# Scores of eight heads at a time, and the attention products of the batch before in front

## The chip, the cores and the metric

The kernel runs on one core of a Trainium2 chip. A core has a matmul engine (TensorE, PE in the profile, with weight loads as PEld), a vector engine (VectorE, DVE), a scalar engine (ScalarE, ACT), a general one (GpSimd, POOL) and a queue that only issues transfers (SyncE, SP). Each engine takes its own instructions in order and waits on semaphores for what others produce. The metric is the time of one execution in microseconds (us), as the median of several runs. Instruction durations come from one profiled execution of the same program.

## The reference

There are 32 batches. Each has 100 rows of x with 256 features, and a context of 361 rows with 256 features. One layer is computed, in fp32 where not said otherwise.

```
xn  = layernorm(x)
Qh, Kh, Vh = xn WQ, ctx WK, ctx WV          # 16 heads of 64
attn = softmax(Qh Kh^T / 8 + mask * -1e9)   # mask 100 x 361, one for all batches
x   = x + concat_heads(attn Vh) WO
x   = x + qlinear(gelu(qlinear(layernorm(x), W1, b1)), W2, b2)
```

`qlinear` rounds its input to 8 bits with one scale and zero point taken over the whole tensor, and its weight to 8 bits with one scale. Hence the second part of the kernel can't begin before all 32 batches have left attention. F, the hidden width, is 1024.

## The kernel before

The program has two parts: attention over 32 batches one after the other, and then the FFN over all rows. The change is in attention alone.

**Tiling.** A "pair" is two heads: 128 rows of queries or keys. A batch has 8 pairs. Eight batch groups (g) of four batches (j = 0 to 3, b = 4g + j) share what is done once a group: the normalized rows (`ln1`, `ln1_T`), the queries (`q_part`, 32 matmuls at the end of j=3), the output projection of the group before (`project_T`, 32 matmuls at the end of j=0), and its transposing back (`project_back`, at the end of j=1 and j=2, followed on VectorE by the residual, statistics and extremes, and on GpSimd by a power and a store). `normalize` of these rows comes one batch later. In the last group each batch but the first is projected on its own (`project`).

**One batch's path.** `products` (L435) multiplies queries and keys of a head into a PSUM bank; two heads of a pair use two halves of the array's rows. `minima` (L449, VectorE) adds the mask, writes the scores to `pb` and finds each row's minimum (queries carry a minus sign). `exponentials` (L463, ScalarE) exponentiates in place and sums. `divide` (L471, L478, VectorE) multiplies by the reciprocal sums, four heads a call. `send` (L503, L512) has GpSimd copy a pair into one of two `apart` buffers with the 16-bit halves of each number taken apart, and SP issue a transposing DMA from there to one of three xT buffers. `join` (L519, ScalarE) puts the halves together again as pT. `attend` (L540) multiplies pT and the values, 96 small matmuls a batch, pair after pair, and ScalarE copies out its two banks (L547). `k_part` (L280, copied by ScalarE at L287) makes the next batch's keys of a pair, `v_part` (L311, copied by VectorE at L318) a third of half of this batch's values.

**Buffers.** PSUM is a ring of eight banks: each score product, key pair, value third and half of `attend` takes the next one, and waits until the one eight places earlier has been read. `pb` holds eight heads. pT, the keys and the values have one buffer each a batch.

**Order.** `whole_batch` is called for batches 1 to 30, and lists by hand the order for TensorE, VectorE, ScalarE and GpSimd; SP's order is found by the framework's planner. The first and the last batch go in parts (`part_of_batch`), transposing on TensorE (`weights_T`). Before the change a whole batch is four quarters (q) of two pairs: scores, minima, exponentials and the keys of two pairs of the next batch. The last join of the batch before stands in quarter 0, its `attend` behind quarter 1, and the values in quarters 2 and 3; the joins of a batch come two quarters behind its sends, the third one after `rest`, which holds the group's work named above. Pieces of the FFN's weight quantization (`todo`) are added in batches 1 to 10: two loads by DMA issued from GpSimd, maxima, rounding.

**Start.** GpSimd clears the last rows of the two `apart` buffers (L205) before it issues two small loads and computes the inverse deviations (L334, L335) that `ln1(0)` needs. VectorE scales two copies of the mask by 1e9 (L675, L676): one for batches in parts, `maskh`, and one for whole batches, `maskt`.

Of the kernel before, what the change touches and what calls it, by code (L numbers as in the profile page):

```python
# [12 lines left out]
ALU = mybir.AluOpType  # L13
# [14 lines left out]
def kernel(  # L28
# [133 lines left out]
    with ExitStack() as att:  # L162
# [38 lines left out]
            wpool.tile([TR, 2 * NSC * 2 * SC], I16, tag=f"apart{k}", name=f"apart{k}")  # L201
            for k in range(2)
        ]
        for t in apart:
            nc.gpsimd.memset(t[T // 32 * 32 :], 0.0)  # L205

        def bank(name):
            return psum.tile([P, 512], F32, tag="ps", name=name)
# [55 lines left out]
        def whole(i):  # L264
            return steps[i][2] == NHP
# [99 lines left out]
        def q_part(g, q):  # L365

            if g >= NG:
                return
            for pair in range(PAIRS):
                pq = bank(f"pq{g}_{q}_{pair}")  # L370
                for dc in range(NDC):
                    nc.tensor.matmul(  # L372
                        pq[:, :GT],
                        wqt[q][:, dc, pair * P : (pair + 1) * P],
                        xnTs[g][:, dc, :],
                        start=(dc == 0),
                        stop=(dc == NDC - 1),
                    )
                j0, j1 = 0, G
                if pair == 0 and g == NG - 1:  # L380
                    clear(q, G - 1)
                for j in range(G):
                    if halved(g * G + j):
                        j0, j1 = (1, G) if j == 0 else (0, j)
                        for k in range(2):
                            nc.vector.tensor_scalar(
                                qbuf[q][:, pair, j, k * RH : k * RH + TH],
                                pq[:, j * T + k * TH : j * T + (k + 1) * TH],
                                -1.0 / DK**0.5, None, ALU.mult,
                            )  # L390
                nc.vector.tensor_scalar(
                    qbuf[q][:, pair, j0:j1, :T],
                    pq[:, j0 * T : j1 * T].rearrange("p (j t) -> p j t", t=T),
                    -1.0 / DK**0.5, None, ALU.mult,
                )
# [30 lines left out]
        def products(i, pairs):  # L426


            b = steps[i][0]
            n = TP if halved(b) else T  # L430
            pss = {}
            for h in range(2 * pairs[0], 2 * pairs[-1] + 2):
                pair, k = divmod(h, 2)
                pss[h] = bank(f"sc{i}_{h}")[:n, :S]
                nc.tensor.matmul(  # L435
                    pss[h],
                    qbuf[pair // PAIRS][k * DK : (k + 1) * DK, pair % PAIRS, b % G, :n],
                    kT[k * DK : (k + 1) * DK, pair, :],
                    start=True,
                    stop=True,  # L440
                )
            return pss

        def minima(i, pss):

            for h, ps in pss.items():
                n = ps.shape[0]
                ms[h] = small.tile([TP, 1], F32, tag=f"m{h}", name=f"m{i}_{h}", bufs=1)
                done = nc.vector.tensor_tensor_reduce(  # L449
                    pb[:n, h % NB, :S], ps, maskh if halved(steps[i][0]) else maskt, 1.0, BIG,  # L450
                    ALU.add, ALU.min, ms[h][:n],
                )
            return done
# [13 lines left out]
        def divide(i, heads, at_once=4, after=None):  # L467
            rsum, r = sums[i]
            n = TP if halved(steps[i][0]) else T
            for h0 in heads[::at_once]:  # L470
                last = nc.vector.reciprocal(  # L471
                    r[:n, h0 : h0 + at_once], rsum[:n, h0 : h0 + at_once]
                )
                if after is not None:
                    follow(last, after)
                for h in range(h0, h0 + at_once):
                    s = pb[:n, h % NB, :S]
                    nc.vector.tensor_scalar(s, s, r[:n, h : h + 1], None, ALU.mult)  # L478
            return last
# [34 lines left out]
        def join(i, q):  # L514
            for pair in range(q * PAIRS, (q + 1) * PAIRS):
                pT = pTs[i, pair] = p1.tile(
                    [SC, 2 * NSC, T], F32, tag=f"pT{pair}", name=f"pT{i}_{pair}"
                )
                nc.scalar.copy(  # L519
                    pT.bitcast(I16).rearrange("s c (t l) -> s c t l", l=2),  # L520
                    xTs[i, pair][:, :, :T].rearrange("s (c l) t -> s c t l", l=2),
                )
# [150 lines left out]
        for b in range(G):  # L673
            stats1(b)
        nc.vector.tensor_scalar(maskh, maskh, 1e9, None, ALU.mult)  # L675
        nc.vector.tensor_scalar(maskt, maskt, 1e9, None, ALU.mult)  # L676
        warm(bank("warm0"), 7)
        k_start()
        for h in range(2):
# [2 lines left out]
        ln1(0)  # L682
        ln1_T(0)
        q_part(0, 0)

# [27 lines left out]
        def part_of_batch(i):  # L715


            b, first, n = steps[i]
            g, j = b // G, b % G
            begun = [h for h in range(2) if first <= h * HP < first + n]  # L720
            ended = [h for h in range(2) if first < (h + 1) * HP <= first + n]
            first_copied = None
            last = scores(i)
            if i >= 1:
                if whole(i - 1):
                    join(i - 1, NQ - 1)
                attend(i - 1)
            if b >= 1:
                for h in begun:
                    for c in range(NSC):  # L730
                        done = v_part(b, h, c)
                        if h == begun[0] and c == 0:
                            first_copied = done
                        if c != 2:
                            copied = done
            while later and i < len(steps) - 1:
                normalize(later.pop(), copied)
            if b == 0 and first < HP:
                for q in range(1, 2) if first == 0 else range(2, NQ):
                    q_part(0, q)  # L740
            rest(i, ended, last, first_copied)
            if g == NG - 1 and j >= 1 and 1 in begun:
                project(b - 1, range(NHP))
            if i + 1 < len(steps):
                for pair in range(steps[i + 1][2]):
                    k_part(i + 1, pair)

        def whole_batch(i):

            b = steps[i][0]
            g, j = b // G, b % G
            late = []
            if not whole(i - 1):
                for pair in range(steps[i - 1][1], steps[i - 1][1] + steps[i - 1][2]):
                    weights_T(i - 1, pair, True)
            for q in range(NQ):
                heads = range(2 * PAIRS * q, 2 * PAIRS * (q + 1))
                minima(i, products(i, range(q * PAIRS, (q + 1) * PAIRS)))  # L760
                if q == 1:
                    divide(i, range(2 * PAIRS))
                    send(i, 0)
                exponentials(i, heads)
                if q == 0 and b - 1 + NCB < B:
                    load_ctx(b - 1 + NCB)
                n = steps[i + 1][2] // NQ
                for pair in range(q * n, (q + 1) * n):
                    k_part(i + 1, pair)
                if q == 0 and whole(i - 1):  # L770
                    join(i - 1, NQ - 1)
                if q == 1:
                    attend(i - 1)
                    last = divide(i, heads)
                    send(i, 1)
                    for piece in todo[:2]:
                        if piece is not None:
                            w, p = piece
                            late.append(quantize_weight(*weights[w], w, p, last))
                    del todo[:2]  # L780
                if q >= 2:
                    join(i, q - 2)
                    for c in range(NSC):
                        v_part(b, q - 2, c)
                        if c == 0:
                            divide(i, heads)
                            send(i, q)
                if q == 2:
                    for f in late:
                        if f is not None:  # L790
                            f()
                    while later:
                        normalize(later.pop(), None)
                    if j == G - 2:
                        ln1(g + 1)
            rest(i, range(2), None)
            join(i, NQ - 2)
            if g == NG - 1 and j >= 1:
                project(b - 1, range(NHP))

# [352 lines left out]
```

## Time and profile before

| what | us |
|---|---|
| median of 3 runs (1283.68 to 1287.6) | 1286.41 |
| the profiled execution | 1286.68 |
| its span, first to last instruction | 1284.4 |
| TensorE busy | 1251.3 |
| VectorE busy | 864.9 |
| ScalarE busy | 818.9 |
| GpSimd busy | 515.0 |
| matmuls of keys, L280 (x1016) | 341.4 |
| matmuls of values, L311 (x768) | 340.1 |
| scores, L435 (x1024) | 191.8 |
| `attend`, L540 (x3072) | 141.7 |

In the span, the whole batches run from about 60 to 1150 us. A group of four takes about 147 us. The mean granted TensorE clock is 0.993 of full. A line of groups in the page gives the source line, engine, operation, output and input, count, busy time, mean of one in ns, and the idle time before it with what ended that. A line of the timeline gives start, length, engine, line, operation, and in brackets the idle time before it with what ended it; matmul lengths include a tail that overlaps the next, so a block's cost is read from start to start.

### The profile page before, as it was taken

To read this page: it belongs to the slowest core of one execution; us is meant where nothing else is said; L and a number is where in the kernel's file an instruction comes from. 1 tells how busy PE (TensorE), PEld (TensorE's weight loads), DVE (VectorE), ACT (ScalarE), POOL (GpSimd) and SP (SyncE) were. 2 spreads that over 40 slices of the span, in tenths; PEclk is the share of its full clock that TensorE was granted. 3 is DMA by queue.
4 is the path that set the end of the run, shared out by engine and by line. 5 is a ranking of instruction groups with operands and counts; after the bars stand their busy time and mean duration, and the time that the engine had idled before them with its cause. 6 is when DMAs were issued, how large, how long until landed. Compare 5 with 4: busy or idle time off the path is not lost.

```text
span 1284.4 us, 21400 instructions
## 1 busy us (share of the span) xinstructions
PE 1251.3 (97%) x7182; PEld 704.0 (55%) x7184; DVE 864.9 (67%) x2403; ACT 818.9 (64%) x1721; POOL 515.0 (40%) x672
## 2 busy tenths in 40 slices
PE   9999999989999999999999999999999999999758
PEld 4655555555555555555555555555555555556426
DVE  5577574776557765786647764786647774686897
ACT  2567566665576855674666855675657754774866
POOL 2044333462435532553435532554335523462260
PEclk9999999999999999999999999999999999999989
DMA  8165534373435543555435534555445533550212
GB/s 260 30 131 98 99 61 82 77 143 77 88 65 96 114 80 66 103 103 98 83 70 105 101 73 73 102 104 102 65 77 104 105 67 77 95 95 17 63 44 103
DMA packets 355204, 115.50 MB, mean 90 GB/s; under 512 B 332078, under 2 KB 353142, under 8 KB 355094
## 3 DMA queue, kind: packets, MB, share of 16 engines
q1 hardware_dynamic: 352016, 107.42, 43.6%
q0 software_dynamic: 2144, 5.38, 1.4%
q10 hardware_dynamic: 934, 1.34, 0.4%
q8 instruction: 56, 0.92, 0.3%
q14 instruction: 54, 0.44, 0.1%
HBM read 24.97 MB, written 6.55 MB: 25 GB/s over the span
## 4 chain that ended last, share of the span: by engine, by line
PE 86%; DVE 5%; issue 3%; POOL 3%; ACT 3%; DMA 0%; POOLq 0%; DVEq 0%; ACTq 0%
PE pk L280 24%; PE pv L311 23%; PE sc L435 13%; PE av L540 10%; PE pq L372 7%; PE py L577 6%; PE pf L1097 2%; ACT h L1007 1%; DVE p L478 1%; DVE v L318 1%; PE po L561 1%; POOL r L944 1%; POOL r L945 1%; POOL apart L503 0%; DMA xT<-apart 0%
## 5 line engine op out<-in xcount | busy, mean ns | idle before, releaser
L503 POOL COPY apart<-p 100x768 int16<-100x768 int16 x480 | 397.7, 863 | 609.6 <-DVE p L478 405.7
L463 ACT ACTIVATE p<-p,m 100x361 f32<-100x361 f32 (+1 forms) x512 | 299.1, 588 | 253.3 <-DVE m L449 252.7
L280 PE MATMUL pk<-c,wkt 128*128 128x361 f32 x1016 | 341.4, 479 | 0.0
L311 PE MATMUL pv<-wvt,c 128*128 128x512 f32 x768 | 340.1, 592 | 0.0
L519 ACT COPY pT<-xT 128x1200 int16<-128x1200 int16 x240 | 309.9, 1336 | 35.2 <-DMA xT<-apart 35.1
L449 DVE CUSTOM_DVE_ANT_0 p<-sc,maskt 100x361 f32<-100x361 f32 x480 | 227.2, 529 | 131.7 <-PE sc L435 119.8
L478 DVE TENSOR_SCALAR p<-p,r 100x361 f32<-100x361 f32 (+1 forms) x512 | 264.5, 579 | 4.4
L280 PEld LDWEIGHTS pk<-c,wkt 128*128 128x128 f32 x1016 | 183.0, 189 | 151.9 <-issue 46.1
L311 PEld LDWEIGHTS pv<-wvt,c 128*128 128x128 f32 x768 | 145.8, 190 | 167.6 <-issue 146.6
L318 DVE COPY v<-pv 128x512 f32<-128x512 f32 x192 | 127.3, 682 | 138.2 <-PE pv L311 137.9
L435 PE MATMUL sc<-kT,q 64*100 64x361 f32 (+1 forms) x1024 | 191.8, 484 | 0.4
L540 PEld LDWEIGHTS av<-pT,v 128*64 128x64 f32 x3072 | 134.5, 138 | 22.6 <-issue 6.1
L540 PE MATMUL av<-pT,v 128*64 128x100 f32 x3072 | 141.7, 252 | 4.3 <-ACT kT L287 4.2
L435 PEld LDWEIGHTS sc<-kT,q 64*100 64x100 f32 (+1 forms) x1024 | 78.2, 163 | 92.4 <-issue 16.8
L287 ACT COPY kT<-pk 128x361 f32<-128x361 f32 x254 | 102.2, 448 | 27.9 <-PE pk L280 27.9
L463 ACT ACTIVATION_READ_ACCUMULATOR p<-p,m 100x1 f32 (+1 forms) x512 | 96.4, 188 | 0.0
L372 PE MATMUL pq<-xnT,wqt 128*128 128x400 f32 x256 | 87.9, 500 | 0.2 <-ACT xnT L363 0.2
L577 PE MATMUL py<-aT,wot 128*128 128x400 f32 x224 | 76.4, 499 | 0.0
L372 PEld LDWEIGHTS pq<-xnT,wqt 128*128 128x128 f32 x256 | 48.4, 190 | 38.8 <-issue 3.3
L577 PEld LDWEIGHTS py<-aT,wot 128*128 128x128 f32 x224 | 42.6, 190 | 34.0 <-issue 3.3
L584 ACT COPY yT<-py 128x400 f32<-128x400 f32 x14 | 6.9, 492 | 84.8 <-PE py L577 84.8
L471 DVE RECIPROCAL r<-rsum 100x4 f32<-100x4 f32 (+2 forms) x131 | 22.4, 172 | 57.0 <-ACT p L463 56.7
(137 smaller groups left out, 730.5 us busy)
## 6 DMA issues: line engine op xcount, KB each, us to landing
c<-in_ctxT_dram SPq DMA_DIRECT2D x31, 361.0 KB
xT<-apart SPq DMA_TRANSPOSE x240
x<-in_x_dram SPq DMA_DIRECT2D x8, 400.0 KB
xb<-xb POOLq DMA_DIRECT2D x32, 100.0 KB, 2.2
x<-xb SPq DMA_DIRECT2D x5, 384.0 KB
out_dram<-ot SPq DMA_DIRECT2D x3, 384.0 KB
wqt<-in_wq_dram SPq DMA_DIRECT2D x4, 256.0 KB
wot<-in_wo_dram SPq DMA_DIRECT2D x1, 1024.0 KB
```

The costliest lines, as they stand in the source:

```text
L280: nc.tensor.matmul(pk[:, :S], wkt[q][:, dc, col * P : (col + 1) * P], c[:, dc, :S], start=(dc == 0), stop=(dc == NDC - 1),)
L311: nc.tensor.matmul(pv[:SC, :], c[:, dc, s * SC : (s + 1) * SC], wvt[h][:, dc, :], start=(dc == 0), stop=(dc == NDC - 1),)
L318: return nc.vector.tensor_copy(vs[b, h][:, s, :], pv[:SC, :])
L372: nc.tensor.matmul(pq[:, :GT], wqt[q][:, dc, pair * P : (pair + 1) * P], xnTs[g][:, dc, :], start=(dc == 0), stop=(dc == NDC - 1),)
L435: nc.tensor.matmul(pss[h], qbuf[pair // PAIRS][k * DK : (k + 1) * DK, pair % PAIRS, b % G, :n], kT[k * DK : (k + 1) * DK, pair, :], start= ...
L449: done = nc.vector.tensor_tensor_reduce(pb[:n, h % NB, :S], ps, maskh if halved(steps[i][0]) else maskt, 1.0, BIG, ALU.add, ALU.min, ms[h] ...
L463: nc.scalar.activation(s, s, AF.Exp, bias=ms[h][:n], scale=-1.0, accum_out=sums[i][0][:n, h : h + 1])
L478: nc.vector.tensor_scalar(s, s, r[:n, h : h + 1], None, ALU.mult)
L503: nc.gpsimd.tensor_copy(src[:T, k * n : (k + 1) * n].rearrange("t (c l s) -> t c l s", c=NSC, l=2), pb[:T, (2 * pair + k) % NB, :].bitcast ...
L519: nc.scalar.copy(pT.bitcast(I16).rearrange("s c (t l) -> s c t l", l=2), xTs[i, pair][:, :, :T].rearrange("s (c l) t -> s c t l", l=2),)
L540: nc.tensor.matmul(av[k * DK : (k + 1) * DK, (pair - p0) * T : (pair - p0 + 1) * T], vs[b, pair // HP][:, c, h * DK : (h + 1) * DK], pTs[i ...
L577: nc.tensor.matmul(py[:, :GT], wot[:, c, dc * P : (dc + 1) * P], aT[:, c, :, :].rearrange("p j t -> p (j t)"), start=(c == 0), stop=(c == ...
```

## The change

In a whole batch, the four quarters become two halves. First comes the load of a context and `attend` of the batch before, then in each half: scores and minima of eight heads, six exponentials, two key pairs, two exponentials, two key pairs, the divisions and sends of four pairs, one join, and three thirds of values. The joins of the third and fourth quarter follow after the loop, one before and one after `rest`, so no join is left for the next batch. `normalize`, `ln1` and the pieces of weight quantization go behind the first half's values. Outside, the clearing of `apart` and the scaling of `maskt` move behind `q_part(0, 0)`, and `part_of_batch` loses its join of the batch before.

```
-        for t in apart:
-            nc.gpsimd.memset(t[T // 32 * 32 :], 0.0)
...
-        nc.vector.tensor_scalar(maskt, maskt, 1e9, None, ALU.mult)
         warm(bank("warm0"), 7)
...
         q_part(0, 0)
+        nc.vector.tensor_scalar(maskt, maskt, 1e9, None, ALU.mult)
+        for t in apart:
+            nc.gpsimd.memset(t[T // 32 * 32 :], 0.0)
...
             if i >= 1:
-                if whole(i - 1):
-                    join(i - 1, NQ - 1)
                 attend(i - 1)
...
-            for q in range(NQ):
-                heads = range(2 * PAIRS * q, 2 * PAIRS * (q + 1))
-                minima(i, products(i, range(q * PAIRS, (q + 1) * PAIRS)))
-                if q == 1:
-                    divide(i, range(2 * PAIRS))
-                    send(i, 0)
-                exponentials(i, heads)
-                if q == 0 and b - 1 + NCB < B:
-                    load_ctx(b - 1 + NCB)
-                n = steps[i + 1][2] // NQ
-                for pair in range(q * n, (q + 1) * n):
+            if b - 1 + NCB < B:
+                load_ctx(b - 1 + NCB)
+            attend(i - 1)
+            for half in range(2):
+                groups = range(half * NQ // 2, (half + 1) * NQ // 2)
+                heads = range(half * NHP, (half + 1) * NHP)
+                minima(i, products(i, range(half * HP, (half + 1) * HP)))
+                n = steps[i + 1][2] // 2
+                keys = range(half * n, (half + 1) * n)
+                exponentials(i, heads[:6])
+                for pair in keys[: n // 2]:
                     k_part(i + 1, pair)
-                if q == 0 and whole(i - 1):
-                    join(i - 1, NQ - 1)
-                if q == 1:
-                    attend(i - 1)
-                    last = divide(i, heads)
-                    send(i, 1)
+                exponentials(i, heads[6:])
+                for pair in keys[n // 2 :]:
+                    k_part(i + 1, pair)
+                for q in groups:
+                    last = divide(i, range(2 * PAIRS * q, 2 * PAIRS * (q + 1)))
+                    send(i, q)
+                join(i, half)
+                for c in range(NSC):
+                    v_part(b, half, c)
+                if half == 0:
+                    while later:
+                        normalize(later.pop(), None)
+                    if j == G - 2:
+                        ln1(g + 1)
                     for piece in todo[:2]:
...
                     del todo[:2]
-                if q >= 2:
-                    join(i, q - 2)
-                    for c in range(NSC):
-                        v_part(b, q - 2, c)
-                        if c == 0:
-                            divide(i, heads)
-                            send(i, q)
-                if q == 2:
-                    for f in late:
-                        if f is not None:
-                            f()
-                    while later:
-                        normalize(later.pop(), None)
-                    if j == G - 2:
-                        ln1(g + 1)
+            for f in late:
+                if f is not None:
+                    f()
+            join(i, NQ - 2)
             rest(i, range(2), None)
-            join(i, NQ - 2)
+            join(i, NQ - 1)
```

## The prediction

> **What bounds the kernel now.** I read the page first: busy shares, the chain that ended last, the costliest groups.
>
> ```profile
> PE 1251.3 (97%) x7182; PEld 704.0 (55%) x7184; DVE 864.9 (67%) x2403; ACT 818.9 (64%) x1721; POOL 515.0 (40%) x672
> ...
> PE 86%; DVE 5%; issue 3%; POOL 3%; ACT 3%; DMA 0%; POOLq 0%; DVEq 0%; ACTq 0%
> ...
> L519 ACT COPY pT<-xT 128x1200 int16<-128x1200 int16 x240 | 309.9, 1336 | 35.2 <-DMA xT<-apart 35.1
> ```
>
> TensorE is busy 97% of the span and is 86% of the chain. So the change can gain only what TensorE spends between useful columns, and loses whatever makes TensorE wait. Next the timeline of TensorE in one batch and in the early parts:
>
> ```profile
> 355.92 1.46 PE L435 MATMUL sc<-kT,q 64*100 64x361 f32 x8
> 357.31 2.69 PE L280 MATMUL pk<-c,wkt 128*128 128x361 f32 x8
> 359.94 1.46 PE L435 MATMUL sc<-kT,q 64*100 64x361 f32 x8
> ```
>
> ```profile
> 45.13 2.65 PE L435 MATMUL sc<-kT,q 64*114 64x361 f32 x16
> 47.72 1.25 PE L540 MATMUL av<-pT,v 128*64 128x100 f32 x24
> 48.90 9.97 PE L280 MATMUL pk<-c,wkt 128*128 128x361 f32 x32
> 58.80 1.70 PE L409 MATMUL pt<-ident,p 50*128 50x50 f32 x48
> ```
>
> Read starts: four heads of scores hold TensorE 1.39 us (355.92 to 357.31), eight in a row 2.59 (45.13 to 47.72), not 2.78. Last, the timeline around the only TensorE wait in the whole batches:
>
> ```profile
> 275.48 1.33 ACT L519 COPY pT<-xT 128x1200 int16<-128x1200 int16 x1 [4.09 <-DMA xT<-apart]
> ...
> 279.53 6.00 PE L540 MATMUL av<-pT,v 128*64 128x100 f32 x96 [4.22 <-ACT kT L287]
> ```
>
> and the busy time of its stretches and of two later ones (columns: stretch, length, busy us of PE, PEld, DVE, ACT, POOL, granted clock, DMA share, GB/s):
>
> ```profile
> 276.57:279.98 3.41, 0.45 (x10) 0.45 (x12) 1.70 (x7) 3.41 (x12) 3.00 (x6) 1.00 0.66 144
> 279.99:283.40 3.41, 3.41 (x48) 3.41 (x44) 0.81 (x3) 3.41 (x7) 3.03 (x6) 0.50 0.20 56
> ...
> 1225.47:1228.88 3.41, 1.17 (x5) 0.39 (x4) 3.41 (x3) 3.41 (x4) 3.32 (x3) 1.00 0.25 58
> 1228.89:1232.30 3.41, 3.19 (x18) 1.92 (x19) 3.41 (x3) 2.77 (x4) 1.28 (x2) 0.50 0.69 211
> ```
>
> A late transpose held `attend` 4.22 us, and its 96 matmuls then took 6.00 us instead of 4.28 (363.95 to 368.23), at half clock.
>
> **Part 1, longer runs of one kind (gain).** Per batch, scores: 4 x 1.39 = 5.56 becomes 2 x 2.59 = 5.18. Keys: blocks of 8 matmuls take 2.63, 2.62, 2.53, 2.53 (the shorter before values); of the 32 in a row above, each further 8 cost (9.90 - 2.53)/3 = 2.46, so two blocks of 16 take 2 x 4.99 = 9.98 against 10.31. Sum 0.38 + 0.33 = 0.71 us; 30 whole batches: **-21.3**.
>
> **Part 2, `attend` first (cost).** It was behind half of the next batch's scores and keys, 2 x (1.39 + 2.63) = 8.0 us; now only values and `rest` stand between. Follow the second half of a batch, 0 being its first score matmul on TensorE. TensorE: scores to 2.6, keys to 7.6, values (12 matmuls, 5.2) to 12.8, then `rest`. VectorE: first minimum at 1.0 (336.01 to 337.00), one each 0.455, done 4.6. ScalarE: first exponential 1.57 (337.58), 0.58 each: six to 5.05, two key copies to 5.7, two exponentials to 6.9, two key copies to 8.2 (the last key product ends near 7.7), then `join` of pairs 2 and 3, 1.24 apart, first done 9.4. VectorE divides heads 8 to 11 from 4.85, heads 12 to 15 after the last exponential, from 7.5. GpSimd copies a head in 0.88 while VectorE divides, else 0.8; pair 4 is ready 7.2, pair 5 8.9. From issue of a transpose to its user:
>
> ```profile
> 300.97 3.99 SPq L512 DMA_TRANSPOSE xT<-apart  x2
> ...
> 304.47 1.33 ACT L519 COPY pT<-xT 128x1200 int16<-128x1200 int16 x1 [1.09 <-DMA xT<-apart]
> 304.54 1.60 POOL L503 COPY apart<-p 100x768 int16<-100x768 int16 x2 [0.97 <-DMA xT<-apart]
> ```
>
> That is 3.5 us to ScalarE, 3.57 to GpSimd. Pair 5 needs the xT buffer of pair 2 (three buffers), so it is issued at 9.5. Pairs 6 and 7 need the two `apart` buffers back: pair 4 lands 10.7, pair 6 is copied (1.6) and issued 12.4, joined by 17.4; pair 5 lands 13.1, pair 7 is issued 14.8, lands 18.4, joined by **19.9**. `attend` takes 0.52 us a pair and could begin pair 7 at 3.7 after its start.
>
> By place j in a group of four batches: j=3 is covered by 32 query matmuls (10.75 us), j=0 by 32 output matmuls (10.75; ScalarE copies their results first, then the joins, some 0.4 us before they are needed). Both cost 0, because of that cover. At j=1 `rest` has four short transposes (0.44): pair 7 is wanted at 12.8 + 0.44 + 3.7 = 16.9, **3.0** late. At j=2, normalize (2 x 0.33) and `ln1` (1.37) now stand on VectorE between the values' copies of the first half and the minima of the second, which start at 2.85, not 1.0. The fifth key bank waits for the first minimum (3.45 instead of 2.6): 0.9 us of TensorE; the chain above runs 1.3 later, TensorE 0.9 + 1.13 of `rest`: 2.7 late. Together **3.6**. What queues behind: eight scores, so the minima and all of the next batch move by the same time. In the last group the projection of a batch stands in front and covers. So 7 groups: 7 x 3.0 + 7 x 3.6 = **+46.2**, plus 0.4 at the first whole batch (no `rest` there) and 0.8 at its front, where `attend` follows its own transposes' copies at once: **+47.4**. Bounds: with the shortest copies on GpSimd and no wait for xT, 2.1 and 2.9 (+35); with the context load, whose issue (0.87) SP now can place ahead of pair 7, in flight (a transpose issued at 306.16 took 4.2), 3.6 and 4.2 (+55). I stay at the middle.
>
> **The clock.** The Trainium skill ("TensorE: Matmul & The Clock Gate", Part 1) gives half clock after a whole idle window of about 3.4 us. My waits are two pieces, some 0.9 for pair 6 and 2.0 for pair 7 with work between, so by the page they cost nothing. The stretches above disagree: windows with 0.45 and even 1.17 us of work were followed by clock 0.50, for 3.41 us, worth 6.00 - 4.28 = 1.7 us. Whether one of mine falls in a window with 2.2 us idle depends on phase: a third of 14, **+8** (by the page 0, by the row each time 24).
>
> **Part 3, small moves.** The load of the second FFN weight (GpSimd, issued 260.86) delayed the transposes behind the 4.22 us wait and the 1.7 after it. It now comes behind the first half's sends, where only pair 3's transpose meets it: **-5.9** (0 if it still meets a needed one). Start: GpSimd's memsets and DMA issues hold back the rsqrt of the first rows:
>
> ```profile
> 12.72 2.90 POOL L205 MEMSET apart<- 16x1536 int16 x2
> ...
> 17.07 0.27 POOL L334 TENSOR_SCALAR v<-mv 100x4 f32<-100x4 f32 x1
> ...
> 19.23 1.53 PE L360 MATMUL ptx<-ident,xn 100*128 100x100 f32 x8 [0.71 <-DVE xn L344]
> ```
>
> Statistics are done at 14.4; without 2.9 us of memsets that step starts near 14.5. TensorE is at the values until 18.5, so only its 0.71 wait and the piecemeal arrival (1.53 against 0.85 at 265.78) go: **-1.5** (0 to -2). The memsets and the mask's scaling (1.52) land where GpSimd and VectorE idle, well before the first send near 77; without that cover, 1.5. The bias loads' issues come 2.9 earlier, for no one. The two joins moved from the next batch are the ones counted above; late weight pieces keep their work, at most 0.7 on ScalarE in four batches.
>
> **Sum.** 1286.68 (its span 1284.4 and 2.3 around it) - 21.3 + 47.4 + 8 - 5.9 - 1.5 = **1313.4**. The profiled execution is 0.3 above the median of 1286.41; I say 1313.
>
> **Rivals.** *Faster:* pair 7 comes in time. Place: the two `apart` buffers and three xT buffers; if their chain were 3 us shorter, no wait and no clock loss: 1286.7 - 28.7 = 1258. It decides where waits and clock together fall below 28.7, or 2.0 us for each of 14. For it: GpSimd is 40% busy and TensorE almost never waited so far. Against: 2.1 and 2.9 are already with everything favourable. *Clock each time* and the context load always in front: +24 and +55: 1337. *ScalarE becomes the bound:* `join` of pairs 0 and 1 now stands in front of the second half's exponentials, done at 13.9 after the first half's scores, wanted 14.4. Transposes at 4.5 instead of 3.5 make every second half 0.5 to 1 late: some 30 x 0.9 = 27 more, 1340. Against: 64% busy, and most landings are near 3.5.
>
> **How the numbers follow.** Mine 0.58; clock and load each time 0.17; ScalarE 0.08; faster 0.14; gains and waits cancelling within 0.3% (about what a measurement of this kernel can tell from no change) 0.03. Slower 0.58 + 0.17 + 0.08 = 0.83. The range leaves out the faster rival and the far end of ScalarE's: low 1292 (waits at 2.1 and 2.9, no clock loss gives 1293), high 1340.
>
> **What would show it.** Right: scores in blocks of 16 at 2.6 us; waits before `av` naming pT or ScalarE at j=1 and j=2 of about 3 us, none at j=0 and j=3; half clock in some; no 4.22 us wait near 276. Wrong: `av` without idle at j=1, or waits before scores and exponentials in every half, or the query and output batches waiting too.

## The result and the profile after

The changed kernel takes 1360.33 us (median, 1355.36 to 1362.68) against 1285.62 for the kernel before: a ratio of 1.0573, 95% interval 1.0552 to 1.0594. It is slower, as forecast, but by 74.7 us where I had said 27, and outside the range. The profiled execution took 1355.36 us, 68.7 more than the one profiled before; the sums below are made against that. In the changed kernel's listing the line numbers of the loop are two lower than before: scores are L433, keys L278, values L309, `attend` L538, `join` L517, `minima` L447. From its page:

```profile
PE 1257.6 (93%) x7184; PEld 725.7 (54%) x7184; DVE 885.1 (65%) x2403; ACT 836.2 (62%) x1721; POOL 519.3 (38%) x672
...
PE 74%; DMA 8%; DVE 5%; issue 4%; ACT 4%; POOL 4%; POOLq 0%; SPq 0%; DVEq 0%; ACTq 0%
...
L278 PE MATMUL pk<-c,wkt 128*128 128x361 f32 x1016 | 325.2, 473 | 7.7 <-DVE m L447 7.7
...
L538 PE MATMUL av<-pT,v 128*64 128x100 f32 x3072 | 153.3, 257 | 59.4 <-ACT pT L517 59.3
```

TensorE fell from 97% to 93%, and DMA, 0% of the chain before, is 8% of it. In the loop two groups of TensorE's instructions have idle time in front: 59.3 us before `attend` (waiting for pT), 7.7 us before keys (waiting for minima). The timeline of TensorE from the second half of batch 13 (j=1) on shows where:

```profile
547.17 2.68 PE L433 MATMUL sc<-kT,q 64*100 64x361 f32 x16
549.78 5.12 PE L278 MATMUL pk<-c,wkt 128*128 128x361 f32 x16
554.74 5.31 PE L309 MATMUL pv<-wvt,c 128*128 128x512 f32 x12
559.88 0.60 PE L589 MATMUL po<-ident,yT 128*100 128x128 f32 x4
560.41 3.31 PE L538 MATMUL av<-pT,v 128*64 128x100 f32 x72
564.45 0.74 PE L538 MATMUL av<-pT,v 128*64 128x100 f32 x12 [0.72 <-ACT pT L517]
567.40 1.27 PE L538 MATMUL av<-pT,v 128*64 128x100 f32 x12 [2.21 <-ACT pT L517]
568.60 5.07 PE L433 MATMUL sc<-kT,q 64*100 64x361 f32 x16
```

Eight heads take 2.61 us from start to start (547.17 to 549.78), as forecast (2.59). `attend` waits for pair 6 and for pair 7, 2.93 us together. Then everything is slow: pair 7 takes 1.20 us from start to start (567.40 to 568.60) instead of 0.52, the scores 5.0 instead of 2.6. The view of stretches (length; busy us of PE, PEld, DVE, ACT, POOL; granted clock; DMA share; GB/s) says why:

```profile
563.22:566.63 3.41, 1.24 (x24) 0.85 (x20) 1.18 (x5) 1.79 (x2) 2.95 (x6) 1.00 0.79 203
566.63:570.04 3.41, 2.64 (x18) 1.79 (x20) 0.00 (x0) 1.60 (x3) 1.92 (x3) 0.50 0.10 32
570.04:573.46 3.42, 3.42 (x14) 1.34 (x10) 2.78 (x11) 2.62 (x9) 0.00 (x0) 0.50 0.02 5
600.76:604.17 3.41, 1.64 (x34) 1.25 (x30) 0.00 (x0) 1.33 (x1) 2.70 (x6) 1.00 1.05 180
604.18:607.59 3.41, 0.56 (x12) 0.54 (x12) 0.00 (x0) 1.72 (x2) 0.57 (x1) 1.00 0.36 102
607.59:611.00 3.41, 3.41 (x17) 1.73 (x14) 1.39 (x5) 1.52 (x4) 0.00 (x0) 0.50 0.00 0
...
1071.80:1075.21 3.41, 1.37 (x32) 1.18 (x28) 0.37 (x2) 0.70 (x1) 3.00 (x6) 1.00 0.75 202
1075.22:1078.63 3.41, 1.64 (x16) 1.33 (x18) 0.00 (x0) 2.33 (x3) 0.78 (x2) 0.50 0.49 131
```

A stretch with 1.24 or 1.37 us of TensorE work is followed by half clock, one with 1.64 is not (its successor, with 0.56, brings it). And the half clock stays for a second stretch where the wait reaches into the first (2.64 of 3.41 us busy). All 14 waits at j=1 and j=2 of the first seven groups set it off: 14 spells, 21 stretches, 71.7 us at half clock, in which TensorE was busy for 59.6 us. At full clock that work would have taken half as long, so 29.8 us are lost. The mean granted clock of the other three executions, 0.962 to 0.967 against 0.968 here, says that it was not the chance of one execution.

The time of a batch, from its first score to the next batch's, means of groups 1 to 6 in us:

```
place      before   after
j=0         41.39   40.64
j=1         31.08   35.39
j=2         32.53   38.88
j=3         42.57   42.04   (before: 41.4 to 41.8 in all but the one with the stall near 276, 48.0)
```

At j=0 nothing waits, so this row shows the gain alone: 0.75 us a batch. A wait at j=1 lies in its own row, but its half clock mostly in the row of j=2, and that of j=2 in the row of j=3. The 68.7 us then come to:

| term | forecast | in the profiles |
|---|---|---|
| longer runs of one kind | -21.3 | -22.5 (30 x 0.75, from j=0) |
| TensorE's waits | +47.4 | +67.0 (59.3 + 7.7) |
| half clock behind them | +8 | +29.8 |
| the old stall and its half clock | -5.9 | -5.9 (4.2 + 1.7) |
| start | -1.5 | -0.3 |
| sum | +26.7 | +68.1 |

The terms are estimates from the traces. Idle time alone makes a wait some 0.3 us too short, since the tail of the matmul before it counts as busy, and the old stall cost its batch 6.6 us and not 5.9; that the sum comes within 0.6 us of 68.7 is in part chance.

### The profile page after: what moved, and what is told of

Its sections match the earlier page's. It is cut to its first block, busy times and chain, and to the rows that moved or that the text cites. A ratio compares the mean times of both kernels' runs of the same rounds, so it can differ in the third digit from the quotient of the medians.

```text
span 1353.4 us, 21435 instructions
## 1 busy us (share of the span) xinstructions
PE 1257.6 (93%) x7184; PEld 725.7 (54%) x7184; DVE 885.1 (65%) x2403; ACT 836.2 (62%) x1721; POOL 519.3 (38%) x672
## 4 chain that ended last, share of the span: by engine, by line
PE 74%; DMA 8%; DVE 5%; issue 4%; ACT 4%; POOL 4%; POOLq 0%; SPq 0%; DVEq 0%; ACTq 0%
PE pk L278 21%; PE pv L309 20%; PE sc L433 11%; DMA xT<-apart 7%; PE av L538 7%; PE pq L370 6%; PE py L575 6%; ACT pT L517 2%; PE pf L1092 2%; POOL apart L501 1%; DVE p L476 1%; DVE v L316 1%; DVE p L447 1%; ACT h L1002 1%; PE po L559 1%
## 5 line engine op out<-in xcount | busy, mean ns | idle before, releaser
L501 POOL COPY apart<-p 100x768 int16<-100x768 int16 x480 | 403.7, 876 | 672.9 <-DVE p L476 527.6
L517 ACT COPY pT<-xT 128x1200 int16<-128x1200 int16 x240 | 315.3, 1335 | 210.3 <-DMA xT<-apart 210.3
L447 DVE CUSTOM_DVE_ANT_0 p<-sc,maskt 100x361 f32<-100x361 f32 x480 | 224.3, 530 | 256.0 <-PE sc L433 246.0
L309 PE MATMUL pv<-wvt,c 128*128 128x512 f32 x768 | 340.1, 592 | 0.0
L278 PE MATMUL pk<-c,wkt 128*128 128x361 f32 x1016 | 325.2, 473 | 7.7 <-DVE m L447 7.7
L476 DVE TENSOR_SCALAR p<-p,r 100x361 f32<-100x361 f32 (+1 forms) x512 | 293.6, 634 | 4.4
L278 PEld LDWEIGHTS pk<-c,wkt 128*128 128x128 f32 x1016 | 188.1, 190 | 142.9 <-DVE m L447 40.2
L309 PEld LDWEIGHTS pv<-wvt,c 128*128 128x128 f32 x768 | 145.8, 190 | 167.6 <-issue 138.9
L538 PE MATMUL av<-pT,v 128*64 128x100 f32 x3072 | 153.3, 257 | 59.4 <-ACT pT L517 59.3
L433 PE MATMUL sc<-kT,q 64*100 64x361 f32 (+1 forms) x1024 | 193.8, 521 | 0.0
L538 PEld LDWEIGHTS av<-pT,v 128*64 128x64 f32 x3072 | 138.6, 141 | 79.6 <-ACT pT L517 66.3
L285 ACT COPY kT<-pk 128x361 f32<-128x361 f32 x254 | 108.4, 450 | 55.3 <-PE pk L278 54.8
L433 PEld LDWEIGHTS sc<-kT,q 64*100 64x100 f32 (+1 forms) x1024 | 91.2, 183 | 91.0 <-issue 41.2
L545 ACT COPY aT<-av 128x400 f32<-128x400 f32 (+2 forms) x67 | 31.6, 474 | 64.9 <-PE av L538 64.9
L389 DVE TENSOR_SCALAR q<-pq 128x400 f32<-128x400 f32 (+1 forms) x64 | 35.0, 546 | 36.2 <-PE pq L370 36.2
```

The costliest lines, as they stand in the source:

```text
L278: nc.tensor.matmul(pk[:, :S], wkt[q][:, dc, col * P : (col + 1) * P], c[:, dc, :S], start=(dc == 0), stop=(dc == NDC - 1),)
L309: nc.tensor.matmul(pv[:SC, :], c[:, dc, s * SC : (s + 1) * SC], wvt[h][:, dc, :], start=(dc == 0), stop=(dc == NDC - 1),)
L433: nc.tensor.matmul(pss[h], qbuf[pair // PAIRS][k * DK : (k + 1) * DK, pair % PAIRS, b % G, :n], kT[k * DK : (k + 1) * DK, pair, :], start= ...
L447: done = nc.vector.tensor_tensor_reduce(pb[:n, h % NB, :S], ps, maskh if halved(steps[i][0]) else maskt, 1.0, BIG, ALU.add, ALU.min, ms[h] ...
L501: nc.gpsimd.tensor_copy(src[:T, k * n : (k + 1) * n].rearrange("t (c l s) -> t c l s", c=NSC, l=2), pb[:T, (2 * pair + k) % NB, :].bitcast ...
L517: nc.scalar.copy(pT.bitcast(I16).rearrange("s c (t l) -> s c t l", l=2), xTs[i, pair][:, :, :T].rearrange("s (c l) t -> s c t l", l=2),)
```

## Experiments

Theory A: the loss is `attend` waiting for the transposes of pairs 6 and 7, and the half clock that these waits bring. Rivals: eight heads at once bunch the work of the other engines, which would cost wherever `attend` stands; the clock is harmless; transposes land late whatever the buffers.

**1. `attend` behind the first half's keys,** as an edit of the changed kernel.

```
-            attend(i - 1)
             for half in range(2):
...
+                if half == 0:
+                    if whole(i - 1):
+                        join(i - 1, NQ - 1)
+                    attend(i - 1)
...
-            join(i, NQ - 1)
```

> The changed kernel, but the last join and attend of the batch before stand behind the first half's keys instead of in front of its scores; halves of eight heads are kept. Theory A (the loss is attend waiting for the transposes of pairs 6 and 7, and the half clock that these waits bring): no waits before av at j=1 and j=2, no half clock in the whole batches, the gain of the longer runs stays (30 x 0.74 = 22) and the kernel before's own 4.2 us wait and 1.7 us of half clock are gone too, the keys' wait of 7.7 us at j=2 stays: 1286 - 22 - 6 + 8 = 1266 us (1260 to 1273). Theory B (eight heads at once bunch the work of VectorE, ScalarE and GpSimd, and that is the loss): the waits move to other places and the time stays over 1320 us.

Measured: 1297.39 us, ratio 1.0103 (1.0064 to 1.0142). Most of the loss is gone, and the waits before `attend` with it (0.7 us are left); but the 1266 us were not reached. The timeline of all engines at the start of batch 14 (j=2) of this kernel shows what `attend` in front had covered:

```profile
548.52 0.39 DVE L599 CUSTOM_DVE_ANT_0 x<-x,po 100x256 f32<-100x256 f32 x1
...
548.97 0.85 PE L433 MATMUL sc<-kT,q 64*100 64x361 f32 x2 [0.45 <-DVE rmax L599]
...
549.81 0.53 DVE L447 CUSTOM_DVE_ANT_0 p<-sc,maskt 100x361 f32<-100x361 f32 x1
...
550.40 1.31 PE L278 MATMUL pk<-c,wkt 128*128 128x361 f32 x2 [0.58 <-DVE m L447]
```

VectorE is still at the residual and statistics of `rest` (3.7 us for two batches' rows, 546.12 to 549.81) when the next scores are ready, so scores wait for banks and keys for minima. TensorE's waits are 23.5 us instead of the 7.7 expected (one of 5.9 us in batch 7, right after batch 6, in which the second weight is loaded and one transpose took 14.6 us), three spells of half clock cost 8.0, and the gain at j=0 is 0.55 us a batch instead of 0.75. I put this last part down to `attend`, which now stands between keys and values; no run shows it. That is 16 + 8 + 6 = 30 of the 31 us missing. The rival's "bunching" exists, then, but it is worth some 24 us here, a third of the loss. One of the three spells follows this same place, though TensorE was busy for 2.37 us of the stretch ahead of it:

```profile
547.29:550.70 3.41, 2.37 (x11) 0.89 (x8) 3.27 (x13) 0.32 (x1) 2.55 (x6) 1.00 1.19 237
550.70:554.11 3.41, 3.41 (x7) 1.89 (x6) 3.37 (x17) 3.41 (x13) 2.98 (x5) 0.50 0.37 87
```

**2. The waits filled.** Matmuls whose results nobody reads, in `attend` of the changed kernel, after batches at j=1 and j=2 of the first seven groups:

```
                 for pair in range(p0, p0 + m):
+                    for _ in range((fill or {}).get(pair, 0)):
+                        nc.tensor.matmul(
+                            av[:, m * T :], idle[:, :P], idle[:, : 512 - m * T], start=True, stop=True
+                        )
...
+            attend(i - 1, fill={6: 20, 7: 48} if waits else None)
```

> The changed kernel with 20 idle matmuls (112 columns, bf16, into unused columns of the bank) before pair 6 and 48 before pair 7 of attend, only after batches at j=1 and j=2 of the first seven groups; some 3.8 us of work in the place of waits of 3.7 to 6.1 us. Theory A: the waits for pair 7 end no earlier, but TensorE keeps the full clock: the 28 us that the half clock costs are gone, the rest of the loss stays: 1330 to 1340 us, granted clock 0.99. Theory C (the clock costs nothing, the waits are all): 1360 us or more.

Measured: 1343.06 us, ratio 1.0477 (1.0436 to 1.0517). TensorE's timeline after batch 13 of this kernel, and its clock:

```profile
552.86 3.31 PE L542 MATMUL av<-pT,v 128*64 128x100 f32 x72
556.10 1.16 PE L536 MATMUL av<-idle 128*128 128x112 bf16 x20
557.19 0.73 PE L542 MATMUL av<-pT,v 128*64 128x100 f32 x12
557.86 2.53 PE L536 MATMUL av<-idle 128*128 128x112 bf16 x48
560.32 0.74 PE L542 MATMUL av<-pT,v 128*64 128x100 f32 x12
560.98 2.68 PE L433 MATMUL sc<-kT,q 64*100 64x361 f32 x16
```

```profile
core 0: 1336.6 us, clock 0.993
```

Useless work in the waits makes the kernel 17 us faster. Pair 7 and the scores behind it run at their usual 0.7 and 2.6 us. In the loop 3.4 us at half clock remain of 71.7, so 28.1 us are recovered. The fillings (14 times 3.55 us, start to start) and the 17.7 us of waits left are 8.1 us more than the 59.3 us that they replace, and keys wait 3.6 longer: 28.1 - 8.1 - 3.6 = 16.4, against 16.8 between the profiled spans. I had expected the fillings to cost nothing, hence 1330 to 1340. The rival "the clock is harmless" falls.

**3. One more buffer of each kind, and the context load out of the way,** in the changed kernel. The lines that shrink the FFN's weights to make room are left out:

```
-            for k in range(2)
+            for k in range(3)
...
-                src = apart[pair % 2]
+                src = apart[pair % 3]
...
-        xTs, NX = {}, 3
+        xTs, NX = {}, 4
...
-                load_ctx(b - 1 + NCB)
+                load_ctx(b - 1 + NCB, behind=sent.get(i - 1))
```

> The changed kernel with three apart buffers instead of two, four xT buffers instead of three, and the context load placed behind the transpose of pair 7 on SP. To make room only the first quarter of each FFN weight is loaded, and all pieces of its quantization use that quarter, so the FFN's weights are not the reference's. Theory A: pair 7 is issued 12.5 us after the second half's first score (14.8 before), joined by 17.4; waits of some 0.5 us at j=1 and j=2, no half clock: 1286 - 22 - 6 + 7 + 8 = 1273 us (1265 to 1290). Theory D (the landing of transposes is slow by itself, buffers don't matter): over 1345 us.

Measured: 1285.95 us, ratio 1.0008 (0.9998 to 1.0019). In batch 13 pair 7 is issued 12.56 us after the second half's first score, lands in 3.44 and is joined at 17.41, where 12.5 and 17.4 were expected. The chain of work that ended last, and TensorE, in this kernel:

```profile
532.12 3.44 DMA xT<-apart
...
535.63 1.35 ACT pT L521
...
537.03 0.74 PE av L542 x12
```

```profile
537.03 0.74 PE L542 MATMUL av<-pT,v 128*64 128x100 f32 x12 [0.39 <-ACT pT L521]
```

The wait of 2.93 us has become 0.39; all waits before `attend` are 16.5 us instead of 59.3 (some 7 were expected), and there is no half clock in the loop. 74 us vanish, `attend` still in front. This kernel loads only a quarter of each FFN weight, so a part could be that. But batches 12 to 27, where none of the three kernels handles a weight, take 582.2 us here, 627.6 in the changed kernel and 585.6 before: the loss is gone there too. So the chain through `apart` and xT, with the load beside it, is what made `attend` late, and the rival "transposes are slow by themselves" falls. Which of the two kinds of buffer counts was not separated.

**4. The context load behind pair 7's transpose, alone.** The last lines of the diff above, nothing else.

> The changed kernel with the context load ordered behind the transpose of pair 7 on SP, nothing else. Theory A with the load's collision as the undersized part: pair 7 lands 3.5 us after its issue instead of 4.0 to 6.4; waits shorter by some 0.8 us in 14 batches, half clock in most of them still: 1340 to 1350 us. If the load doesn't slow the transpose: 1360 us.

Measured: 1341.85 us, ratio 1.0441 (1.0409 to 1.0474), as expected. In the changed kernel SP issues in this order (batch 13):

```profile
559.53 1.37 SPq L510 DMA_TRANSPOSE xT<-apart  x1
560.95 0.86 SPq L211 DMA_DIRECT2D c<-in_ctxT_dram  x1
561.96 1.60 SPq L510 DMA_TRANSPOSE xT<-apart  x1
```

Pair 7's transpose, the third line, landed after 3.98 us; over the 14 places that wait it took 3.4 to 6.4 us, on average 4.6, where pairs 4 to 6 mostly took 3.4 to 3.7. The chain of the changed kernel and that of this one, in batch 13:

```profile
561.96 3.98 DMA xT<-apart
```

```profile
561.52 3.46 DMA xT<-apart
```

With the order reversed TensorE waits for it less:

```profile
564.01 0.74 PE L542 MATMUL av<-pT,v 128*64 128x100 f32 x12 [0.71 <-ACT pT L521]
566.44 1.27 PE L542 MATMUL av<-pT,v 128*64 128x100 f32 x12 [1.70 <-ACT pT L521]
```

All waits are 59.5 us instead of 67.0, half clock 54.6 us instead of 71.7. Less waiting (7.5 us) and less half clock (29.8 to 24.5 us lost) make 12.8 us, against 11.6 between the profiled spans; the medians differ by 18.5. So the load ahead of pair 7 is a part of the loss, not all of it: without it pair 7 still took over 5 us in batches 2 and 22, and pair 6 up to 5.

**5. `attend` in front, alone,** in the kernel before with its four quarters:

```
+            attend(i - 1)
             for q in range(NQ):
...
-                if q == 0 and whole(i - 1):
-                    join(i - 1, NQ - 1)
                 if q == 1:
-                    attend(i - 1)
...
             join(i, NQ - 2)
+            join(i, NQ - 1)
```

> The kernel before in its four quarters, with only attend of the batch before in front of the first quarter and the last join at the end of the batch; no longer runs of one kind, start unchanged. Theory A (attend in front is the loss): no gain of 22 us; here the third join stands behind the output projection's copies and pair 7's transpose behind that join, so j=0 waits too: waits of 3 us and more at j=0, j=1 and j=2 and half clock behind most of them: 1375 to 1420 us. Theory B (the eight heads are a part of the loss): below the changed kernel's 1360 us, towards 1300.

Measured: 1420.32 us, ratio 1.1047 (1.1019 to 1.1076), just past the upper end of the expectation. TensorE waits 89.4 us before `attend` and runs at half clock for 109.2 us. So the halves of the change are not its loss; they take 60 us off what `attend` in front costs. Some 22 of these are the gain at j=0, 22 are shorter waits (67.0 against 89.4), and 10 are less work at half clock (29.8 us lost against 39.5). Why the waits are shorter I put down, without a run of its own, to sends that come earlier in a batch and to j=0, where this kernel waits too (44.75 us a batch against 40.64). After a j=1 batch:

```profile
420.53 0.74 PE L540 MATMUL av<-pT,v 128*64 128x100 f32 x12 [0.51 <-ACT pT L519]
423.74 0.74 PE L540 MATMUL av<-pT,v 128*64 128x100 f32 x12 [2.47 <-ACT pT L519]
426.25 1.27 PE L540 MATMUL av<-pT,v 128*64 128x100 f32 x12 [1.77 <-ACT pT L519]
```

**6. The start alone,** in the kernel before, with the memsets forced behind the second step of the inverse deviation (the moves of the lines are left out):

```
-            nc.gpsimd.memset(t[T // 32 * 32 :], 0.0)
+            follow(nc.gpsimd.memset(t[T // 32 * 32 :], 0.0), powers[0])
```

> The kernel before with only the start's part of the change, and the two memsets ordered behind the power on GpSimd. Theory E (the planner put one memset between the two steps of the inverse deviation, so the start gained 0.3 us instead of 1.5): the transposes of the first rows start at 18.5 us instead of 19.2 (18.9 in the changed kernel), the queries some 1.4 us earlier than before (19.6 instead of 21.0), the loop as before: 1283 to 1286 us. If VectorE's mask scaling or copies hold the first rows instead: 20.6 us for the queries as in the changed kernel.

One run, 1282.27 us. The expectation failed. The queries start at 20.96 us, as before the change (21.00). In the changed kernel the planner had put one memset between the two steps; here none is between, and the first rows are normalized from 15.77 us on instead of 18.67. But (the kernel before first):

```profile
18.67 1.39 DVE L344 TENSOR_SCALAR xn<-x,mv,rstd 100x256 f32<-100x256 f32 x4 [0.93 <-POOL rstd L335]
```

```profile
15.77 3.33 DVE L342 TENSOR_SCALAR xn<-x,mv,rstd 100x256 f32<-100x256 f32 x3 [1.17 <-POOL rstd L333]
```

```profile
15.79 2.84 POOL L684 MEMSET apart<- 16x1536 int16 x2
```

Four of these instructions take 1.39 us in the kernel before, where GpSimd is at rest. Here the first two, beside GpSimd's memsets, take 1.55 and 1.54 us, and the other two 0.40 each. What the earlier start gives is lost again on VectorE. (The span is 4.0 us shorter than before for another reason: the stall near 276 us is 2.0 us here instead of 4.2, and no half clock follows. One run of 1282 us lies inside the scatter of the kernel before, so only the trace speaks here.)

**7. What was left of experiment 1 spread out,** as an edit of that kernel: half of `rest` moves to the end of the first half, `normalize` and `ln1` go ahead of the values, and the second weight is loaded one batch later.

```
+                if half == 0:
+                    while later:
+                        normalize(later.pop(), None)
+                    if j == G - 2:
+                        ln1(g + 1)
                 for c in range(NSC):
                     v_part(b, half, c)
                 if half == 0:
+                    rest(i, range(1), None)
...
-            rest(i, range(2), None)
+            rest(i, range(1, 2), None)
...
+        todo[10:10] = [None, None]
```

> The kernel with attend behind the first half's keys (the first experiment), with its remaining waits taken away: the half of rest that belongs to h=0 stands at the end of the first half, normalize and ln1 stand before the first half's value copies, and the second FFN weight is loaded one batch later (j=3). The first experiment's waits of 23.8 us and its half clock of 8 us fall to some 4 us together; the longer runs keep 0.55 us a batch (16.5 in all, attend now stands between keys and values) and the 5.9 us of the kernel before's own wait and clock are gone: 1268 us (1262 to 1278). If the bunching on VectorE and ScalarE remains and only moves: 1290 or more.

Measured: 1272.48 us, ratio 0.9902 (0.9874 to 0.993): by 1% faster than the kernel before. TensorE at j=2 in this kernel:

```profile
513.77 2.68 PE L433 MATMUL sc<-kT,q 64*100 64x361 f32 x16
516.70 5.12 PE L278 MATMUL pk<-c,wkt 128*128 128x361 f32 x16 [0.25 <-DVE m L447]
521.66 5.31 PE L309 MATMUL pv<-wvt,c 128*128 128x512 f32 x12
526.81 0.38 PE L589 MATMUL po<-ident,yT 128*100 128x128 f32 x2
527.12 2.68 PE L433 MATMUL sc<-kT,q 64*100 64x361 f32 x16
```

The waits in the loop are 9 us in all, and none is followed by half clock. The gain at j=0 is 0.55 us a batch: 30 x 0.55 and the old stall's 5.9, less 9 of waits, make 13.4 us, and 13.0 were measured. So the eight-head halves gain once `attend` stands behind keys and VectorE's side work is spread. The three moves were made together, so what each is worth is not known.

## Why the prediction was wrong

- **Bound and gain: right.** TensorE sets the time, and j=0, where nothing waits, gains 0.75 us a batch (forecast 0.71). That this is all due to longer runs is not shown: `attend` moved too, and with the same halves but `attend` behind the keys the gain is 0.55 (experiments 1 and 7).
- **Places of the waits: right.** They are at j=1 and j=2 of the first seven groups, none at j=0, at j=3 or in the last group, and keys wait only behind `normalize`, `ln1` and, in batch 7, a weight's maxima. Scores wait nowhere in the loop, so the rival in which ScalarE becomes the bound did not come true.
- **The chain up to the issue of pair 7: right where nothing disturbs it.** In batch 16 pairs 4 to 7 are issued at 7.16, 9.58, 12.36 and 14.78 us; the forecast said 7.2, 9.5, 12.4 and 14.8. In batch 13 the wait is 2.93 us against 3.0, but this is in part luck: the load stood in front there too, and pair 7 landed after 3.98 us instead of 3.6. From start to start (560.41 to 567.40, against 3.7 undisturbed) the wait is 3.3 us.
- **Wrong size 1: "I stay at the middle", +47.4.** It measured 67.0. I had named the context load on SP ahead of pair 7 and put it into a bound of 3.6 and 4.2 us. It stood there in every such batch and cost more: before `attend` TensorE waited on average 4.1 us at j=1 (forecast 3.0) and 4.35 at j=2 (forecast 2.7). The keys' wait at j=2 came out as forecast, 0.9; another 1.5 us of it fell in batches 7 and 30. One landing of 4.2 us in the trace before was taken for its worst; it went to 6.4. Putting that load behind removes 7.5 of the 19.6 us (experiment 4). The rest goes with later issues of pairs 5 and 7 (pair 7 at 15.7 on average for j=1, 14.8 forecast), many in the ten batches with weight work, and with other slow landings; its cause stays open.
- **Wrong size 2: "a third of 14, +8".** All 14 fired and cost 29.8, beyond even the "by the row each time 24", because half clock stayed for a second stretch in 7 of the 14 spells, where a part of the wait lay in the first. The trace before had the evidence, a stretch with 1.17 us of work followed by half clock; but I reckoned with phases in which the wait is cut in two harmless parts, and even the shortest wait, the 2.93 us of batch 13, set it off. The Trainium skill's whole idle window ("TensorE: Matmul & The Clock Gate", Part 1) would have given 0 for the waits as forecast. In this trace the stretch ahead of 12 of the 14 spells still held 0.57 to 1.37 us of work, and the other two 0.02 and 0.11; experiment 2 shows that the spells cost 28 us.
- **Start: wrong, small.** -1.5 was forecast, -0.3 came: a memset slipped between the two steps, and VectorE is slower beside the memsets where they now run (experiment 6). I had called that cover free because both engines idle there.
- **The old stall: right in size by the account,** though experiment 6 shows that it is not fixed: 2.0 us in a kernel with the same loop.

So the rival that came true is "clock each time and the context load always in front", to which I gave 0.17, and its 1337 was still short: 29.8 for 24, and 67.0 for 55. I had left the load's place open although in the trace before it already stood between pairs 6 and 7 in all 28 whole batches that load a context, and a chance of a third for the clock had no run behind it.

## What to carry to other kernels

Before a consumer is moved forward, work out the chain of its last input with every buffer that must come free and every transfer that may be issued in between, and take the disturbed landing for the likely one if the queue's order allows it. Where TensorE waits, ask how much of a 3.41 us stretch stays idle: in the changed kernel each of the 14 waits, 2.9 to 6.1 us long, cost itself and on average 2.1 us more (29.8 by 14). A move that brings longer runs can be kept by putting the consumer behind them: here that, with VectorE's side work spread and one weight loaded a batch later, turned +5.7% into -1.0%.

## What the runs showed of the hardware

- In the loop of the changed kernel the granted clock halved after every 3.41 us stretch in which TensorE was busy for 1.37 us or less, and after none with 1.64 us or more. At half clock a stretch with 2.64 us busy was followed by another one.
- Idle time does not tell the whole: in experiment 1 a stretch with 2.37 us busy, most of it scores on 64 rows of the array, was followed by half clock. Why is open.
- A transposing DMA that lands in 3.4 to 3.7 us took 4.0 to 6.4 in the 12 batches where a plain load of 361 KB was issued 1.0 to 1.3 us ahead of it, and 3.4 and 3.5 in the two where the load was 2.1 us ahead. With the load behind it (experiment 4) 9 of 14 landed in 3.4 to 3.7 us.
- Beside a GpSimd memset of 1.4 to 1.6 us, VectorE's tensor-by-scalar work in SBUF took about as long as the memset: 1.55 us instead of 0.41 (100 x 256), and 1.52 for the scaling of a mask in the kernel before, 0.35 in the changed one without a memset beside it.
